# A post-norm decoder on one core: first experts' rows scattered to token order, second context early, another order in self-attention rounds

## The chip, the core and the metric

The kernel runs on one core of a Trainium2 chip. The core has engines with queues of their own: TensorE (PE in the profile, its weight loads PEld) for matmuls and transposes, VectorE (DVE), ScalarE (ACT) and GpSimd (POOL) for elementwise work and reductions, and SyncE (SP), which here only issues DMAs. GpSimd issues the indirect DMAs, which gather or scatter rows by an index. The metric is device time in microseconds (us), as the median of several runs. Next to it stands one profiled execution with a record of each instruction.

## The reference

The input is x of 8 x 256 tokens with 256 features and a context of 8 x 77 tokens with 192. Six sublayers follow one another, and after each comes a layer norm of the sum with its input:

```python
x = _layernorm(x + _L0_attn_ref(x, ...))             # gated linear attention
x = _layernorm(x + _L0_xattn_ref(x, ctx_768, ...))   # 16 heads over the context
x = _layernorm(x + _L0_ffn_ref(x, ...))              # 8 experts, 2 for each token
x = _layernorm(x + _L1_attn_ref(x, ...))             # 16 heads, window of 128 on each side
x = _layernorm(x + _L1_xattn_ref(x, ctx_768, ...))   # logits clipped at 10000
x = _layernorm(x + _L1_ffn_ref(x, ...))              # 8 experts with limited room
```

In the first experts each token has two experts with softmax weights, and each computes `(silu(x W1) * (x W2)) W3`. The second experts use `silu(x w1 + b1) w2 + b2`.

## The kernel before

All of x stays on chip as 16 chunks of 128 tokens, two for each batch, with a transposed copy xT. All is fp32 but for masks, one-hots and softmax shifts in bf16.

**Order of work.** An attention stage is a list of (function, ahead, arguments); `round_of(steps, b)` calls each for batch b + ahead, so that one round works on several batches at once. The text sets the order in which instructions are given. The framework then fixes the order in each engine's queue: nearly always that of the text, but an instruction may pass one whose inputs are expected later. Each queue runs in that order, so an instruction that waits holds up all behind it. PSUM has eight buffers, shared by all stages (`ps`).

**First experts, `ffn0`.** Routing sorts the 2 x 2048 choices by expert into 39 blocks of 128 rows (NB0). For block i, `fetch` gathers its rows from DRAM on GpSimd four blocks ahead, `turn_rows` transposes them (pt_g), `hidden` makes p_u and p_v (L1013), `turn_hidden` transposes their product (pt_h), and `output` makes p_y (L1035) one block later. VectorE copies it to yo (L1040, three buffers), and SyncE stores it to the DRAM tensor ys at the block's place (L1041).

**Back to tokens, `combine`.** For a batch, four gathers on GpSimd (L896) fetch from ys the rows of two chunks and two choices; VectorE multiplies each by its weight and adds (yc, L909). `norm` takes statistics on VectorE, adds and raises to the power -0.5 on GpSimd (L112, L113), and scales on VectorE (x, L115). `combine` is a step of the self-attention's rounds, three batches ahead; `turn_batch` (pt_x, L129) makes xT of the batch two ahead.

**Self-attention rounds.** A batch's exponentials need a row maximum first. `maxima` makes scores p_s (L681) on top of a mask (L671) and reduces them on VectorE (m, L687): sixteen reductions for each batch, in four calls. `less_max` splits the negated maxima into bf16 parts, transposes them (p_mx, L459), and `shift` adds them to the transposed scores p_st that `weigh` makes for the exponentials e on ScalarE (L703). `average` multiplies by the values (p_pv), `divide` divides, `turn` and `project` bring back rows, and `norm_batch` adds and norms. `values` makes p_v of the next batch, and VectorE adds the bias into vals (L659). A round below runs from one p_mx to the next.

**Cross-attention, `xattn`.** `context` makes the keys (p_k, four parts; copied by ScalarE at L542 and VectorE at L545) and values (p_v, one part for each batch) of the context, as a step of the rounds two batches ahead. The second one's weights, w_x1, are loaded after the first experts. Its rounds also hold the routing of the next experts: `choose`, `place` and `enter` (p_tok).

**Second experts, `ffn1`.** Here the output already goes by an indirect DMA on GpSimd (L1115) to token order, and plain loads of 512 KB (L1145, SyncE) bring it back once all 20 scatters have landed. Unused places of a block go to rows after the tokens' (`dump`).

## Time and profile before

| what | value |
|---|---|
| median of 3 runs | 1300.39 us (1299.35 to 1302.56) |
| profiled execution, its own time | 1301.57 us |
| its span | 1299.8 us |
| granted TensorE clock, mean | 0.888 of full speed |
| TensorE busy | 1054.2 us, 81% of the span |
| VectorE busy | 655.3 us, 50% |
| ScalarE busy | 448.4 us, 34% |
| GpSimd busy | 339.9 us, 26% |
| last p_y of the first experts starts | 707.10 us |
| first p_mx of the self-attention | 763.38 us |
| first p_mx of the second cross-attention | 1026.86 us |
| first load back in the second experts | 1263.86 us |

The span runs from the first to the last instruction; the execution's own time is a little longer. A row of a timeline gives start, duration, engine, line, operation, what is written and read, and in brackets how long the engine had been idle before it and what ended that. "<-issue" stands for idle time for which the profile shows no wait. An engine's share of the whole span is a mean over stages with different limits, so that a change in one stage is read from that stage.

### The profile page before, as it was taken

The page shows a single profiled execution, that of the slowest core. Times are in us where ns is not written, and L with a number is a line of the kernel's source. Part 1 is how long each engine was busy: PE and PEld are TensorE (multiplying, and loading weights), DVE is VectorE, ACT ScalarE, POOL GpSimd, SP SyncE. Part 2 cuts the span into 40 slices and gives each one's busy share as a digit, 9 for nine tenths or more (in the row PEclk, how much of TensorE's full clock was granted, in tenths as well). Part 3 has the DMA queues.
Part 4 walks back from the last instruction along what each step waited for, and adds up shares of the span by engine and source line. Part 5 has one row for each costly group of instructions (what it writes and reads, how often), then busy time and mean ns, then how long its engine had stood idle before and what let it go on. Part 6 is the DMA issues. An engine that isn't in the chain of part 4 may idle for free.

```text
span 1299.8 us, 25292 instructions
## 1 busy us (share of the span) xinstructions
PE 1054.2 (81%) x10221; PEld 692.1 (53%) x10221; DVE 655.3 (50%) x1833; ACT 448.4 (34%) x874; POOL 339.9 (26%) x454
## 2 busy tenths in 40 slices
PE   6888888888898649999997468888998888873870
PEld 4556665665665426666665235555555555652540
DVE  6667676654555432222222544444444566764325
ACT  3445454424444212212121134333443444330104
POOL 7545555430111021111111730000000110101544
PEclk9789988889999659999999689899999998975895
DMA  7000000003111291111111210000000010105425
GB/s 191 3 2 2 3 3 2 2 3 130 34 33 34 61 303 45 49 41 49 45 45 57 77 49 2 1 1 1 2 1 1 2 33 18 34 24 150 138 82 174
DMA packets 54517, 62.64 MB, mean 48 GB/s; under 512 B 10897, under 2 KB 45858, under 8 KB 54402
## 3 DMA queue, kind: packets, MB, share of 16 engines
q1 hardware_dynamic: 46368, 44.59, 10.6%
q0 software_dynamic: 5616, 15.34, 4.2%
q8 instruction: 82, 1.34, 0.4%
q10 hardware_dynamic: 2418, 1.09, 0.4%
q14 instruction: 33, 0.27, 0.1%
HBM read 42.78 MB, written 18.22 MB: 47 GB/s over the span
## 4 chain that ended last, share of the span: by engine, by line
PE 56%; DVE 24%; ACT 5%; POOL 5%; issue 4%; DMA 4%; SPq 0%; POOLq 0%; ACTq 0%; DVEq 0%
PE p_y L51 6%; PE p_u L1013 5%; PE p_y L1035 5%; PE p_v L1013 5%; PE p_pv L51 4%; DVE m L687 3%; PE p_q L51 3%; PE p_v L51 3%; PE p_s L681 3%; PE p_st L585 2%; PE p_k L51 2%; PE p_st L696 2%; DVE tot L267 2%; DVE al L275 2%; PE p_s L51 2%
## 5 line engine op out<-in xcount | busy, mean ns | idle before, releaser
L687 DVE TENSOR_REDUCE m<-p_s 128x2 f32<-128x512 f32 x128 | 80.1, 683 | 31.8 <-PE p_s L681 31.8
L1019 DVE TENSOR_TENSOR h<-h,p_v 128x512 f32<-128x512 f32 x39 | 26.8, 688 | 121.1 <-PE p_v L1013 121.1
L896 POOL DMA_INDIRECT xg<-rows,tok x39 | 37.0, 949 | 178.3 <-PE pt_g L1002 158.9
L122 DVE TENSOR_TENSOR y<-p_y,xb 128x512 f32<-128x512 f32 x24 | 16.5, 688 | 118.0 <-PE p_y L51 118.0
L1013 PE MATMUL p_u<-fw,xgT 128*128 x156 | 75.3, 606 | 0.6 <-DVE xgT L1004 0.6
L499 POOL TENSOR_TENSOR xb<-x,L_xattnbo 128x512 f32<-128x512 f32 x16 | 20.3, 1271 | 210.6 <-DVE y L122 169.6
L703 ACT ACTIVATE e<-p_st 128x512 f32<-128x512 f32 x128 | 66.9, 643 | 22.6 <-PE p_st L468 20.2
L1035 PE MATMUL p_y<-fw,hT 128*128 x312 | 73.8, 379 | 0.7 <-ACT hT L1028 0.7
L1013 PE MATMUL p_v<-fw,xgT 128*128 x156 | 74.0, 597 | 0.0
L1035 PEld LDWEIGHTS p_y<-fw,hT 128*128 128x128 f32 x312 | 59.2, 190 | 25.2 <-issue 18.2
L592 ACT ACTIVATE e<-p_st 77x512 f32<-77x512 f32 x128 | 65.7, 600 | 17.7 <-PE p_st L468 17.7
L1028 ACT COPY hT<-pt_h 128x512 f32<-128x512 f32 x39 | 22.8, 585 | 128.7 <-PE pt_h L1026 128.7
L477 ACT COPY u<-p_pv 128x512 f32<-128x512 f32 x48 | 28.1, 585 | 110.9 <-PE p_pv L51 109.9
L51 PE MATMUL p_pv<-e,vals 77*32 77x256 f32 (+1 forms) x1024 | 64.8, 394 | 0.0
L130 ACT COPY xT<-pt_x 128x512 f32<-128x512 f32 x40 | 23.4, 585 | 111.1 <-PE pt_x L129 110.5
L499 POOL TENSOR_TENSOR xb<-x,L_attnbo 128x512 f32<-128x512 f32 x8 | 10.1, 1268 | 189.4 <-DVE y L122 189.4
L129 PE MATMUL pt_x<-ident,x 128*128 128x128 f32 x160 | 28.2, 301 | 37.9 <-DVE x L115 37.5
L576 DVE TENSOR_REDUCE m<-p_s 128x4 f32<-128x308 f32 x128 | 53.0, 467 | 6.9 <-PE p_s L51 6.9
L51 PEld LDWEIGHTS p_pv<-e,vals 77*32 77x32 f32 (+1 forms) x1024 | 33.5, 112 | 32.0 <-issue 18.2
L1013 PEld LDWEIGHTS p_v<-fw,xgT 128*128 128x128 f32 x156 | 30.1, 193 | 38.2 <-issue 38.2
L681 PE MATMUL p_s<-kT,qT 32*128 32x512 f32 x256 | 50.0, 696 | 0.0
L260 POOL TENSOR_TENSOR kl<-kT,be 128x256 f32<-128x256 f32 x56 | 48.2, 861 | 4.4
(271 smaller groups left out, 2420.1 us busy)
## 6 DMA issues: line engine op xcount, KB each, us to landing
fw<-in_L_ffn_W SPq DMA_DIRECT2D x24, 512.0 KB
rows<-x SPq DMA_DIRECT2D x32, 256.0 KB
ys<-yo SPq DMA_DIRECT2D x39, 128.0 KB
m<-in_L_ffn_w SPq DMA_DIRECT2D x16, 256.0 KB
z<-ys SPq DMA_DIRECT2D x8, 512.0 KB
x<-in_x SPq DMA_DIRECT2D x8, 256.0 KB
out<-x SPq DMA_DIRECT2D x8, 256.0 KB
b<-in_L_ffn_b ACTq DMA_DIRECT2D x8, 128.0 KB
```

What stands on the lines that cost most here:

```text
L51: nc.tensor.matmul(dst, l, r, start=(i == 0), stop=(i == n - 1))
L129: nc.tensor.transpose(pt[:, dc, c, :], x[:, 2 * b + c, dc * P:(dc + 1) * P], ident)
L260: nc.gpsimd.tensor_tensor(halves(kls[w][b % 2], w)[:, :, 0, :], halves(kT[b], w)[:, :, 0, :], halves(be, w)[:, :, 0, :], ALU.mult,)
L499: nc.gpsimd.tensor_tensor(xb, x[:, 2 * b:2 * b + 2, :], self.bo.unsqueeze(1).broadcast_to([P, 2, D]), ALU.add)
L576: nc.vector.tensor_reduce(st.less(b)[:, c, j, :], p, AX.X, ALU.max, negate=True)
L592: nc.scalar.activation(e[0:KV].rearrange("p i q -> p (i q)"), p[0:KV].rearrange("p i q -> p (i q)"), AF.Exp)
L681: nc.tensor.matmul(tiles[j].rearrange("p a m -> p (a m)"), st.qT[b][r, t, c * P:(c + 1) * P], kTs[b][r, t, :, :].rearrange("p a m -> p (a ...
L687: nc.vector.tensor_reduce(st.less(b)[:, c, j, 2 * t:2 * t + 2], p, AX.X, ALU.max, negate=True)
L703: nc.scalar.activation(e.rearrange("p i q -> p (i q)"), p.rearrange("p i q -> p (i q)"), AF.Exp)
L896: nc.gpsimd.indirect_dma_start(out=out, out_offset=None, in_=table, in_offset=bass.IndirectOffsetOnAxis(ap=index, axis=0),)
L1013: nc.tensor.matmul(p, xg[:, dc, :], w[:, bass.ds(e * (2 * FF) + dc * FF, FF)], start=(dc == 0), stop=(dc == 1),)
L1035: nc.tensor.matmul(y, hT[:, f * P:(f + 1) * P], w3[:, bass.ds(e * (4 * D) + f * D, D)], start=(f == 0), stop=(f == 3),)
```

## The change

**First experts' output.** `output` no longer stores a block at its place, but scatters its rows with GpSimd to token order, as the second experts do. The addresses dst come from tf, the place of each slot in token order, below zero for an unused slot, which goes to a row of `dump`. In `combine` a batch is now one plain load of 512 KB (z, three buffers, five batches ahead), and the four additions follow three batches ahead, as before. Each load waits for all 39 scatters. `scatter`, `load_back` and `returned` are shared with `ffn1`, whose instructions stay the same.

**Second context.** Making keys and values is split from `xattn` as `xcontext`. For the second cross-attention it is called right after the experts, ahead of the self-attention's rounds, and its weights are loaded behind the experts' own; its rounds then have no `context` steps. For the first one the order stays.

**Order of rounds.** In the self-attention the first `maxima` comes before `values`, another before the first `average`, and both calls of `turn_batch` and the last `maxima` before the second `average`. In the second cross-attention `enter` stands before `project` rather than after it.

```diff
--- before.py
+++ after.py
@@ -419,7 +419,7 @@
         r = []
         for i in range(2):
-            m = pool.tile([P, 2, 4, 32], BF16, tag=f"mx{i}", name=f"mx{i}")
+            m = pool.tile([P, 2, 4, 32], BF16, tag=f"mx{i}", name=f"mx{i}", bufs=1)
             nc.gpsimd.memset(m, 0.0)
             r.append(m)
         return r
@@ -520,13 +520,10 @@
             norm_batch(b, py, xb, self.bk)
-    def xattn(w, ctxT, clamp, es):
+    def xcontext(w, ctxT, es):
+
         wkk, bk, wv, bv = w[2:6]
         kvp = es.enter_context(tc.tile_pool(name="x_kv", bufs=1, reuse_waits="tile"))
-        wk = es.enter_context(tc.tile_pool(name="x_wk", bufs=2, reuse_waits="tile"))
-        st = Steps(w, max_buffers(kvp), wk, wk, clamp)
-
-
         keys = kvp.tile([P, 2, B, 2, KV], F32, tag="keys", name="keys")
         vals = kvp.tile([P, B, H, 32], F32, tag="vals", name="vals")
         nc.gpsimd.memset(vals[:, :, :, DH:32], 1.0)
@@ -563,6 +560,14 @@
             elif b in (0, 2):
                 key_part(part, b // 2)
+        return context, keys, vals
+
+    def xattn(w, given, clamp, es):
+
+        context, keys, vals = given
+        wk = es.enter_context(tc.tile_pool(name="x_wk", bufs=2, reuse_waits="tile"))
+        st = Steps(w, max_buffers(wk), wk, wk, clamp)
+
         def maxima(b, c):
             tiles = [ps.tile([P, 4, KV], F32, tag="ps", name="p_s") for _ in range(4)]
             for t in range(2):
@@ -612,11 +617,10 @@
             (st.queries, 1, 1),
             (weigh, 0, 0),
             (st.turn, -1),
-            (context, 2, 0),
-            (context, 2, 1),
+            *([(context, 2, 0), (context, 2, 1)] if context else []),
             (weigh, 0, 1),
             (st.project, -1),
-            (context, 2, 2),
+            *([(context, 2, 2)] if context else []),
             (maxima, 1, 0),
             (average, 0, 0),
             (average, 0, 1),
@@ -726,14 +730,15 @@
             (weigh, 0, 1, 0),
             (st.project, -1),
             (weigh, 0, 1, 1),
+            (maxima, 1, 0, 0),
             (values, 1),
-            (maxima, 1, 0, 0),
+            (maxima, 1, 1, 0),
             (average, 0, 0),
             (maxima, 1, 0, 1),
+            (turn_batch, -1),
+            (turn_batch, 2),
+            (maxima, 1, 1, 1),
             (average, 0, 1),
-            (maxima, 1, 1, 0),
-            (turn_batch, -1),
-            (maxima, 1, 1, 1),
             (st.divide, 0),
             (st.queries, 2, 0),
         ]
@@ -898,20 +903,52 @@
             in_offset=bass.IndirectOffsetOnAxis(ap=index, axis=0),
         )
-    def combine(b, ys, idx, wgt, wk):
-
-        y = wk.tile([P, 2, D], F32, tag="yc", name="yc")
-        for c in range(2):
-            n = 2 * b + c
-            for k in range(2):
-                yg = wk.tile([P, D], F32, tag=f"yg{k}", name=f"yg{k}")
-                gather(yg, ys, idx[:, k, n:n + 1])
-                nc.vector.scalar_tensor_tensor(
-                    y[:, c, :], yg, wgt[:, k, n:n + 1], y[:, c, :] if k else x[:, n, :], ALU.mult, ALU.add
-                )
-        norm(b, y)
-
-    def ffn0(r, w1, w2, w3, ys, meanwhile):
+    def scatter(table, index, rows, sent):
+        s = nc.gpsimd.indirect_dma_start(
+            out=table, out_offset=bass.IndirectOffsetOnAxis(ap=index, axis=0), in_=rows, in_offset=None,
+        )
+        for other in sent:
+            tc.declare_no_dep(s.ins, other.ins, reason="no two slots go to one place")
+        sent.append(s)
+
+    def load_back(z, rows, sent):
+        s = nc.sync.dma_start(out=z, in_=rows)
+        for other in sent:
+            tc.add_manual_dep(
+                s.ins, other.ins.name,
+                mybir.DependencyInfo(mybir.DependencyClass.Sync, mybir.DependencyReason.DATA),
+                reason="any block may have written these rows",
+            )
+
+    def returned(ys, n):
+
+        return ys[0:2 * NT, :].rearrange("(b c k p) d -> b p (c k) d", c=n, k=2, p=P)
+
+    def combine(ys, sent, wgt, wk):
+
+        zs = {}
+
+        def bring(b):
+            zs[b] = wk.tile([P, 4, D], F32, tag="z", name="z", bufs=3)
+            load_back(zs[b], returned(ys, 2)[b], sent)
+
+        def add(b):
+            z = zs.pop(b)
+            y = wk.tile([P, 2, D], F32, tag="yc", name="yc")
+            for c in range(2):
+                n = 2 * b + c
+                for k in range(2):
+                    nc.vector.scalar_tensor_tensor(
+                        y[:, c, :], z[:, 2 * c + k, :], wgt[:, k, n:n + 1], y[:, c, :] if k else x[:, n, :],
+                        ALU.mult, ALU.add,
+                    )
+            norm(b, y)
+
+        return bring, add
+
+    def ffn0(r, w1, w2, w3, ys, dump, meanwhile):
+
+
         rows = r.rows.rearrange("c k p d -> (c k p) d")
         with ExitStack() as es:
             gp = es.enter_context(tc.tile_pool(name="f_g", bufs=1, reuse_waits="tile"))
...
@@ -958,6 +995,8 @@
                     )
             tf = gp.tile([P, NB0], F32, tag="tf", name="tf")
             tok = gp.tile([P, NB0], I32, tag="tok", name="tok")
+            dst = gp.tile([P, NB0], I32, tag="dst", name="dst")
+            none = gp.tile([P, NB0], F32, tag="none", name="none")
             nc.vector.tensor_scalar(tf, pt[:, NB0:2 * NB0], float(P), -float(P), ALU.mult, ALU.add)
             nc.vector.tensor_tensor(tf, tf, pt[:, 0:NB0], ALU.add)
             nc.vector.tensor_scalar(tok, tf, 0.0, None, ALU.max)
@@ -974,11 +1013,11 @@
             nc.vector.tensor_scalar(bi, be, float(NE - 1), None, ALU.min)
-            idx = r.kept([2, NC], "idx", I32)
             wgt = r.kept([2, NC], "wgt")
             def returns():
-                nc.vector.scalar_tensor_tensor(idx, r.blk, float(P), r.row, ALU.mult, ALU.add)
+                nc.vector.scalar_tensor_tensor(none, tf, 0.0, dump, ALU.is_lt, ALU.mult)
+                nc.vector.tensor_tensor(dst, tf, none, ALU.add)
                 d = gp.tile([P, NC, NE], F32, tag="d", name="d")
                 nc.vector.tensor_tensor(d, r.m[:, 0], r.m[:, 1], ALU.subtract)
                 nc.vector.tensor_tensor(d, d, r.lg, ALU.mult)
...
@@ -1038,18 +1077,17 @@
                     )
                 yo = wk.tile([P, D], F32, tag="yo", name="yo")
                 nc.vector.tensor_copy(yo, y)
-                nc.sync.dma_start(out=ys[i * P:(i + 1) * P, :], in_=yo)
+                scatter(ys, dst[:, i:i + 1], yo, sent)
             for i in range(-4, NB0 + 1):
-                if i == 4:
+                if i == 0:
                     returns()
                 for f, n in ((fetch, i + 4), (hidden, i), (output, i - 1), (turn_hidden, i), (turn_rows, i + 2)):
                     if 0 <= n < NB0:
                         f(n)
-            return idx, wgt
+            return wgt, sent
     def ffn1(r, b1, b2, w1, w2, ys, dump):
-
         rows = r.rows.rearrange("c k p d -> (c k p) d")
         with ExitStack() as es:
...
@@ -1218,7 +1243,7 @@
             )
-    ys = dram.tile([2 * NT + NE * CAP, D], F32, tag="ys", name="ys")
+    ys = dram.tile([2 * NT + P * NB0, D], F32, tag="ys", name="ys")
     right, early = ExitStack(), ExitStack()
     with tc.tile_pool(name="x0_w", bufs=1) as xw:
         lent = {}
@@ -1230,7 +1255,7 @@
             lent["wg0"] = load_k(aw, "wg0", a["L0_ffn_Wg"], NE)
             lent["wg1"] = load_k(aw, "wg1", a["L1_ffn_gate_w"], NE)
             lent["b1"] = load(aw, "b1", a["L1_ffn_b1"], [P, NE, 2], "e (f p) -> p e f", p=P)
-            for n, shape in (("upper", [P, P]), ("iota", [P, P]), ("tid", [P, NC]), ("dump", [P, NB1]),
+            for n, shape in (("upper", [P, P]), ("iota", [P, P]), ("tid", [P, NC]), ("dump", [P, NB0]),
                              ("half", [P, 2]), ("chosen", [P, 4])):
                 lent[n] = load(aw, n, a["c_" + n], shape)
             lent["caps"] = load(aw, "caps", a["c_caps"], [P, 2, 2 * NE], "p (k e) -> p k e", k=2)
...
@@ -1274,37 +1299,41 @@
         load_experts(fw2, FF, "L0_ffn_W2", 2)
         load_experts(fw3, D, "L0_ffn_W3", 4)
         w_s1 = attn_weights(late, "L1_attn", False)
+        w_x1 = attn_weights(late, "L1_xattn", True)
         far = load(late, "far", a["c_far"], [P, 2, P], "p (k s) -> p k s", k=2)
         masks = late.tile([P, 2, P], BF16, tag="masks", name="masks")
         def meanwhile():
             quarter(w_s1)
+            quarter(w_x1)
             nc.vector.tensor_copy(masks, far)
-        idx, wgt = ffn0(r0, fw1, fw2, fw3, ys, meanwhile)
+        wgt, sent = ffn0(r0, fw1, fw2, fw3, ys, dump, meanwhile)
     early.close()
-    late = ctx.enter_context(tc.tile_pool(name="x1_w", bufs=1, reuse_waits="tile"))
-    w_x1 = attn_weights(late, "L1_xattn", True)
     with ExitStack() as es:
         ck = es.enter_context(tc.tile_pool(name="c_wk", bufs=2, reuse_waits="tile"))
         fs = ExitStack()
         steps = self_attn(w_s1, masks, es, fs)
-        steps.insert(4, (lambda b: combine(b, ys[0:NB0 * P, :], idx, wgt, ck), 3))
-        steps.insert(len(steps) - 1, (turn_batch, 2))
-        for b in range(-3, B):
+        bring, add = combine(ys, sent, wgt, ck)
+        steps.insert(4, (add, 3))
+        steps.insert(0, (bring, 5))
+        xs = ExitStack()
+        context, *given = xcontext(w_x1, ctxT, xs)
+        for part in range(3):
+            for b in range(B):
+                context(b, part)
+        for b in range(-5, B):
             run(round_of(steps, b))
-        quarter(w_x1)
         fs.close()
         right.close()
         rest = round_of(steps, B)
-        xs = ExitStack()
-        steps = xattn(w_x1, ctxT, 10000.0, xs)
+        steps = xattn(w_x1, (None, *given), 10000.0, xs)
         run(alternate(rest, round_of(steps, -2) + round_of(steps, -1)))
         rp = right.enter_context(tc.tile_pool(name="r1", bufs=1, side="right", reuse_waits="tile"))
         rw = right.enter_context(tc.tile_pool(name="r1_wk", bufs=2, side="right", reuse_waits="tile"))
         r1 = Route(1, wg1, rp, rw)
         steps.insert(len(steps) - 2, (r1.choose, -1))
-        steps.insert(8, (r1.enter, -2))
+        steps.insert(5, (r1.enter, -2))
         steps.insert(3, (r1.place, -2))
         for b in range(B + 2):
             run(round_of(steps, b))
...
```

More of the change, by code (lines that the diff above doesn't have):

```diff
@@ L943, in ffn0 @@
             for k in range(2):
-                ob = gp.tile([P, NC, NB0], BF16, tag=f"ob{k}", name="ob")
+                ob = gp.tile([P, NC, NB0], BF16, tag="ob", name="ob")
                 o2 = gp.tile([P, NC, 2, NB0], BF16, tag=f"o2{k}", name="o2")
@@ L988, in returns @@
                 meanwhile()
-            raw, xgs, hs, hTs = {}, {}, {}, {}
+            raw, xgs, hs, hTs, sent = {}, {}, {}, {}, []
             def fetch(i):
@@ L1061, in ffn1 @@
             nc.vector.tensor_scalar(src, r.table, -float(P), 0.0, ALU.add, ALU.max)
-            nc.vector.scalar_tensor_tensor(none, r.table, 0.0, dump, ALU.is_equal, ALU.mult)
+            nc.vector.scalar_tensor_tensor(none, r.table, 0.0, dump[:, 0:NB1], ALU.is_equal, ALU.mult)
             nc.vector.scalar_tensor_tensor(dst, r.table, -float(P), none, ALU.add, ALU.add)
@@ L1114, in output @@
                     at += n
-                s = nc.gpsimd.indirect_dma_start(
-                    out=ys, out_offset=bass.IndirectOffsetOnAxis(ap=dst[:, i:i + 1], axis=0),
-                    in_=yo, in_offset=None,
-                )
-                for other in sent:
-                    tc.declare_no_dep(s.ins, other.ins, reason="no two slots go to one place")
-                sent.append(s)
+                scatter(ys, dst[:, i:i + 1], yo, sent)
             for i in range(10):
@@ L1137, in ffn1 @@
                         output(5 * g - 5 + h)
-            back = ys[0:2 * NT, :].rearrange("(b c k p) d -> b p (c k) d", c=4, k=2, p=P)
             yc, stats = {}, {}
@@ L1144, in fetch_pair @@
                 for h in range(2):
-                    s = nc.sync.dma_start(out=z[:, 4 * h:4 * h + 4, :], in_=back[g][:, 4 * h:4 * h + 4, :])
-                    for other in sent:
-                        tc.add_manual_dep(
-                            s.ins, other.ins.name,
-                            mybir.DependencyInfo(mybir.DependencyClass.Sync, mybir.DependencyReason.DATA),
-                            reason="any block may have written these rows",
-                        )
+                    load_back(z[:, 4 * h:4 * h + 4, :], returned(ys, 4)[g][:, 4 * h:4 * h + 4, :], sent)
                 y = wk.tile([P, 4, D], F32, tag="yc", name="yc")
@@ L1255, in decoder_kernel @@
         with ExitStack() as es:
-            steps = xattn(w_x0, ctxT, None, es)
+            steps = xattn(w_x0, xcontext(w_x0, ctxT, es), None, es)
             run(alternate(rest, round_of(steps, -2) + round_of(steps, -1)))
@@ L1345, in _constants @@
         "c_chosen": np.stack([(u[:, 0] % 32 < 12) & (u[:, 0] % 4 == i) for i in range(4)], 1).astype(np.float32),
-        "c_dump": (2 * NT + P + np.arange(P)[:, None] + P * np.arange(NB1)[None, :]).astype(np.float32),
+        "c_dump": (2 * NT + P + np.arange(P)[:, None] + P * np.arange(NB0)[None, :]).astype(np.float32),
         "c_tri": np.ascontiguousarray(np.broadcast_to(tri.reshape(1, NE * NE), (P, NE * NE))),
```

## The prediction

> **What bounds the kernel now.** First the slices: the engine rows by stage. Columns: stretch, length, then busy us (instructions) of TensorE, its weight loads, VectorE, ScalarE, GpSimd, then granted clock, DMA share, GB/s.
>
> ```profile
> 675.00:700.00 25.00, 25.00 (x97) 15.96 (x96) 6.84 (x13) 4.73 (x8) 0.00 (x0) 1.00 0.07 22
> ...
> 709.10:723.67 14.57, 0.00 (x1) 0.01 (x1) 4.45 (x12) 0.00 (x0) 8.95 (x11) 0.58 0.28 81
> 723.67:763.38 39.71, 21.19 (x85) 11.19 (x85) 28.57 (x68) 4.52 (x9) 26.46 (x30) 0.71 0.22 63
> ...
> 833.10:867.50 34.40, 30.66 (x278) 18.39 (x278) 15.92 (x39) 13.98 (x28) 3.12 (x5) 0.95 0.00 1
> ...
> 932.68:963.42 30.74, 28.96 (x279) 18.13 (x279) 14.55 (x33) 13.98 (x28) 2.16 (x3) 1.00 0.01 1
> ```
>
> In the first experts TensorE is full. From their last matmul (709.10) it waits 14.57 us; until the first shift transpose p_mx of self-attention (763.38) it is half busy at a clock of 0.71, and GpSimd and VectorE carry the stage. Then eight rounds follow, from p_mx to p_mx 32.1, 37.6, 34.4, 34.4, 30.8, 30.7, 30.7 and 32.7 us. A steady round holds 28.96 us of TensorE; 34.4 has 3.7 idle and 1.7 from the lower clock.
>
> The timeline says what the gap waits for:
>
> ```profile
> 709.13 0.42 DVE L1040 COPY yo<-p_y 128x256 f32<-128x256 f32 x1 [2.74 <-PE p_y L1035]
> 712.28 1.01 POOL L896 DMA_INDIRECT yg<-ys,idx  x1 [5.96 <-issue]
> ...
> 715.39 0.48 DVE L909 SCALAR_TENSOR_TENSOR yc<-yg,wgt,x 128x256 f32<-128x256 f32 x1 [5.83 <-DMA yg<-ys,idx]
> ...
> 723.67 1.12 PE L129 MATMUL pt_x<-ident,x 128*128 128x128 f32 x4 [14.57 <-DVE x L115]
> ```
>
> Store, landing, a gather every 1.25 us, four per batch, then the norm. In the rounds the chain meets VectorE:
>
> ```profile
> 814.42 2.08 PE L51 MATMUL p_v<-L_attnwv,xT 128*128 128x256 f32 x4 [3.85 <-DVE vals L659]
> ...
> 956.96 4.88 DVE L687 TENSOR_REDUCE m<-p_s 128x2 f32<-128x512 f32 x8 [1.03 <-PE p_s L681]
> ...
> 963.42 0.28 PE L459 MATMUL p_mx<-identb,mx 128*128 128x128 bf16 x2 [1.10 <-DVE mx L456]
> ```
>
> The second p_v waits until VectorE, behind a combine, has taken the first; the last eight maxima queue for 4.88 us just ahead of p_mx.
>
> **Part 1: experts' end.** 39 stores by SyncE become 39 scatters by GpSimd. Price, by the second experts and by the gathers:
>
> ```profile
> L896 POOL DMA_INDIRECT yg<-ys,idx x32: 942/946/1208, 712.3 to 767.3; - x32
> L1115 POOL DMA_INDIRECT ys<-yo,dst x20: 965/971/1002, 1223.9 to 1261.2; - x20
> ```
>
> A block (5.8 us) then holds 0.95 + 0.97 = 1.92 us of GpSimd: hidden behind TensorE; without that cover 39 x 0.97 = 38 us. A gather queued behind a scatter now waits for p_y and its copy, and pt_g for that gather; but gathers are issued four blocks ahead, and nothing else is on the queue except memsets (3.7 us, near 704). The copy into yo waits for the scatter three blocks back, 17 us, against a landing under 2.7. Two small VectorE operations for the addresses replace one; without cover 0.5 us. SyncE's 0.9 MB of cross-attention weights move behind the experts' weights, where SyncE is idle afterwards (DMA share 0.07): nothing; without cover 3 us, at the 303 GB/s of the page's fullest slice.
>
> [...] The trace has 971 ns beside VectorE's bias additions and at most 1208 ns for gathers beside the combine. Its copies in this stage read PSUM, 424 ns. I take 0.97 and nothing[...].
>
> **Part 2: the gap.** The last scatter can start where the store did, 709.6. In the second experts the loads start 1263.86, 2.65 us after the last scatter (1261.21): so 712.3, the time of the first gather now. One load there took 3.8 us to its consumer (ScalarE at 1267.75), the next 1.4 and 1.9 more: data at 716.1, 717.5, 719.4 for batches 0, 1, 2. Three buffers: the fourth waits until batch 0 is added; behind it on SyncE are only the later loads. In the old kernel batch 0 was complete at 723.9.
>
> VectorE now has the context as well: 4 key copies at 0.60 and 8 value copies at 0.42 (as in the rows of keys and vals later) = 5.8 us, in among the first additions. So batch 0 is complete near 726.1, **2.3 us later**; batches 1 and 2, no longer paced by four gathers of 1.25 each plus the norm's GpSimd steps, near 731 and 735 (before 732.5 and 741.2). VectorE's load from the end of the experts to p_mx is 33.0 (both rows) + 5.8 = 38.8 us, from about 712.5: not before 751.3. Written out operation by operation I get p_mx at 754.8, against 763.38: **-8.6 us**. From below: if VectorE waits as often as it does now, 0; from above -12.1.
>
> TensorE's clock: [...] the context's 14.6 us of matmuls fill the gap, and if they keep the clock up, p_v, p_s and the masks before p_mx (7.1 us cold on the chain of waits) take half. [...] VectorE ends last anyway. I take nothing and keep -3.5 for the range.
>
> **Part 3: context leaves the second cross-attention.** Costs now on the path:
>
> ```profile
> 1011.01 2.83 PE L51 MATMUL p_k<-ctxT,L_xattnwk 128*128 128x308 f32 x8
> ...
> 1029.23 2.93 PE L51 MATMUL p_k<-ctxT,L_xattnwk 128*128 128x308 f32 x8
> ```
>
> In the transition p_k and two p_v (1.2 each) stand ahead of pt_o, 5.2 us; TensorE idles 3.6 there for other reasons, so **-4**. In its first round p_k goes, but the p_mx after it follows from y and the norm: **-2**. In rounds 1 to 5 one p_v (1.2) goes; they idle 1.7 to 2.6 us, and the path is y, GpSimd's addition and power, x, transpose: between 0 and -6, I take **-1**. The tokens' p_tok in four rounds now precedes p_y and waits for VectorE's one-hot; p_y, y and the norm queue behind it, some 0.85 us each at worst (+3.4), mostly behind GpSimd's 1.27 us addition: **+0.8**.
>
> **Part 4: order of the rounds.** Eight reductions take 5.4 us per round half; moving two groups of maxima forward gives VectorE work while TensorE averages, and spares the last queue. Ceiling: idle and clock loss of each round against 28.96: 3.1, 8.7, 5.4, 5.4, 1.8, 1.8, and 3.4 in the seventh; 29.6 in all. The waits that the order touches: the p_v wait (3.85 and twice 2.0) in rounds with a combine, and p_mx's wait with the issue gaps after it. I take -2.8, -4.4, -3, -3, -1.2, -1.2, -2.2 = **-18** (61% of the ceiling), because values now come behind four more reductions of 0.68 and average may wait for them; if all of it is lost, 0.
>
> **Sum.** -8.6 - 18 - 4 - 2 - 1 + 0.8 = -32.8. The profiled execution took 1301.57 (span 1299.8, 1.8 around it): 1268.8. The median of the runs is 1300.39, 1.2 lower: 1267.6, say **1268 us**. A difference under 0.3% (3.9 us) can't be told from none.
>
> **Rivals.**
> A. The barrier takes the place of the gathers: all 39 scatters must land and the context stands on VectorE ahead of the adds, so p_mx stays at 763. For it: batch 0 is later even in my count. Against: 32 gathers of 0.95 us leave the stretch. 1268 + 8.6 = 1277.
> B. The new order only exchanges waits: values late, average waits, p_mx as before. For it: VectorE's total is unchanged, and steady rounds are 94% TensorE already. Then -15: 1286. Halfway, 1277.
> C. More: warm clock -3.5, the orders' whole ceiling -11.6, values in the cross-attention -5: to 1248.
> D. Slower: GpSimd becomes the pace of the first experts[...]. It decides where scatter plus gather exceed 5.8 us plus the 32.8/39 = 0.84 that the rest gains: 3.3 us each. At 3.5 each: 7.0 - 5.8 = 1.2 x 39 = +47: 1314. Against: no row over 1.21 us.
> E. It doesn't do what it says: scatters still hold the loads up because landing, not issue, is slow with scattered 1 KB rows. Second experts: 2.65 us with the same rows. At most some 3 more, 1271.
>
> **How the numbers follow.** Mine 50%, A 13%, B 17%, C 11%, D 6%, E 3%. Low end between C and mine, 1251; the high end is B, 1286; outside are D and the ends of B and C, some 2 in 10. Faster by over 0.3%: mine, A, C, E and nearly all of B, 0.90; same: the rest of B with bad p_tok, 0.03; slower: D and a little of B, 0.07.
>
> **What would show it.** Experts still end near 709 and GpSimd's row there is about 8 of 25 us. z loads issue near 712, TensorE's idle of 14.57 is filled by p_k and p_v, pt_x of batch 0 comes at 726 and not before 724, p_mx near 755. Rounds with a combine fall to 31 to 33, the steady ones to 29.5. No p_k after 725; the second cross-attention's start comes 4 us sooner after the last self-attention p_mx. Wrong: a scatter row above 2 us, pt_x after 730, a vals row that average waits for, or rounds that keep 30.7.

## The result, and the profile after

The changed kernel takes 1279.14 us in the median of four runs (1277.38 to 1280.60), against 1299.89 us for the kernel before on the same chip: a ratio of 0.9835, with an interval of 0.982 to 0.985. That is 20.8 us less. The forecast was 1268 us, with 1251 to 1286 around it: right in sign and inside the range, but a gain of 32 us was worked out and two thirds of it came. The profiled execution took 1277.38 us with a span of 1275.5, which is 24.3 under the span before; it was the fastest of its four.

The stage ahead of the experts ends anywhere from 473.0 to 480.2 us in the profiles of this document, with the same work. Places are therefore taken between instructions of one execution. Each step of the forecast against the two profiles (the last p_y is the start of its eight matmuls):

| stretch | before, us | after, us | difference | forecast |
|---|---|---|---|---|
| start of the span to the experts' first pt_g | 475.36 | 476.55 | +1.2 | 0 |
| first pt_g to the last p_y | 231.74 | 231.16 | -0.6 | 0 |
| last p_y to the self-attention's first p_mx | 56.28 | 47.79 | -8.5 | -8.6 |
| its seven rounds | 230.78 | 220.41 | **-10.4** | **-18** |
| to the second cross-attention's first p_mx | 32.70 | 28.29 | -4.4 | -4 |
| its first round | 14.69 | 13.12 | -1.6 | -2 |
| its next six rounds | 113.86 | 116.03 | **+2.2** | **-0.2** |
| from there to the end | 144.39 | 142.15 | -2.2 | 0 |

A second profile of the changed kernel, `after_again`, has the same gap and steady rounds, but 223.1 us in the seven rounds (-7.7) and 114.5 in the six (+0.6): these two rows are known to some 3 and 2 us only. The last row is a sum of two unlike parts: x of the last batch comes 4.3 us later, and the second experts then take 4.6 us less from their first pt_g to their last matmul, though no edit touches them.

The rows by stage of the changed kernel, with the columns as before (stretch, length, busy us of TensorE, its weight loads, VectorE, ScalarE, GpSimd, granted clock, DMA share, GB/s):

```profile
675.00:700.00 25.00, 25.00 (x96) 15.74 (x95) 6.83 (x13) 4.73 (x8) 3.89 (x4) 1.00 0.06 22
...
709.70:726.98 17.28, 14.88 (x50) 5.50 (x48) 9.39 (x24) 2.44 (x4) 2.44 (x4) 1.00 0.40 130
726.98:755.50 28.52, 19.00 (x84) 10.25 (x85) 26.13 (x68) 4.52 (x9) 7.07 (x10) 0.83 0.24 74
...
784.44:821.73 37.29, 33.64 (x280) 19.50 (x279) 18.19 (x48) 13.77 (x28) 3.12 (x5) 0.86 0.01 2
821.73:854.88 33.15, 30.53 (x280) 18.83 (x278) 16.17 (x41) 13.77 (x28) 3.12 (x5) 0.95 0.00 1
...
917.47:946.93 29.46, 28.74 (x279) 18.12 (x278) 14.70 (x35) 13.77 (x28) 2.16 (x3) 1.00 0.00 1
```

The experts are still full on TensorE, with the scatters in GpSimd's column. The gap behind them is filled by the context, and from 727 on VectorE is busy for 26.13 of 28.52 us. The steady rounds fell from 30.74 to 29.46. The second round, the longest, is as long as it was (37.6 and 37.3).

The timeline of the gap (start, duration, engine, line, operation, and in brackets the idle time before it and what ended it):

```profile
709.54 5.68 PE L51 MATMUL p_k<-ctxT,L_xattnwk 128*128 128x308 f32 x16
...
710.44 0.98 POOL L907 DMA_INDIRECT ys<-yo,dst  x1 [0.36 <-DVE yo L1079]
...
715.15 9.43 PE L51 MATMUL p_v<-L_xattnwv,ctxT 128*77 128x256 f32 x32
...
719.11 0.47 DVE L941 SCALAR_TENSOR_TENSOR yc<-z,wgt,x 128x256 f32<-128x256 f32 x1
...
726.98 0.67 PE L129 MATMUL pt_x<-ident,x 128*128 128x128 f32 x4 [2.40 <-DVE x L115]
...
755.50 0.37 PE L459 MATMUL p_mx<-identb,mx 128*128 128x128 bf16 x2 [6.05 <-DVE mx L456]
```

This is what was forecast: batch 0 at 726 to 727, later than before, and p_mx near 755. The loads were issued at 713.27. The price of a scatter was right as well; here are all 59 of both expert layers:

```profile
L907 POOL DMA_INDIRECT ys<-yo,dst x59: 965/987/1002, 492.3 to 1237.7; - x59
```

Now the second round, where the forecast had -4.4:

```profile
798.39 0.74 DVE L115 TENSOR_SCALAR x<-y,mv,rs 128x256 f32<-128x256 f32 x2 [0.82 <-POOL rs L113]
...
800.42 0.73 DVE L115 TENSOR_SCALAR x<-yc,mv,rs 128x256 f32<-128x256 f32 x2 [1.13 <-POOL rs L113]
801.19 0.88 DVE L941 SCALAR_TENSOR_TENSOR yc<-z,wgt,x 128x256 f32<-128x256 f32 x2
801.99 0.87 DVE L941 SCALAR_TENSOR_TENSOR yc<-z,wgt,yc 128x256 f32<-128x256 f32 x2
...
802.92 0.67 DVE L691 TENSOR_REDUCE m<-p_s 128x2 f32<-128x512 f32 x1
...
803.64 0.37 PE L675 MATMUL p_s<-masks,identb 128*128 128x256 bf16 x1 [3.64 <-DVE m L691]
...
805.94 2.08 PE L51 MATMUL p_v<-L_attnwv,xT 128*128 128x256 f32 x4
...
809.96 3.66 PE L51 MATMUL p_pv<-e,vals 128*32 128x256 f32 x32
```

The combine (x of one batch, the additions of another) still stands ahead of everything that TensorE needs from VectorE. Before, p_v waited 3.85 us for vals; now the mask of the second `maxima` waits 3.64 us for the first reduction. Then TensorE runs slowly, at a granted clock of 0.50 for ten us (803.64 to 813.70): a p_v takes 2.08 us here, 1.13 ahead of the wait at a clock of 1.00, and p_pv 3.66 against 1.97 behind it.

### The profile page after: what moved, and what is told of

The parts are those of the page before. It is cut to its first block, busy times and chain, and to the rows that moved or that the text cites. A ratio compares the mean times of both kernels' runs of the same rounds, so it can differ in the third digit from the quotient of the medians.

```text
span 1275.5 us, 25238 instructions
## 1 busy us (share of the span) xinstructions
PE 1057.5 (83%) x10221; PEld 690.5 (54%) x10221; DVE 655.6 (51%) x1834; ACT 447.6 (35%) x874; POOL 348.5 (27%) x461
## 4 chain that ended last, share of the span: by engine, by line
PE 57%; DVE 21%; POOL 6%; issue 6%; ACT 5%; DMA 3%; SPq 1%; POOLq 0%; ACTq 0%; DVEq 0%
PE p_u L1052 5%; PE p_y L1074 5%; PE p_v L1052 5%; PE p_y L51 5%; PE p_q L51 4%; PE p_pv L51 3%; PE p_v L51 3%; PE p_st L590 2%; DVE m L691 2%; PE p_k L51 2%; PE p_st L700 2%; PE p_s L685 2%; PE pt_x L129 2%; DVE tot L267 2%; DVE al L275 2%
## 5 line engine op out<-in xcount | busy, mean ns | idle before, releaser
L907 POOL DMA_INDIRECT ys<-yo,dst x59 | 57.9, 981 | 158.1 <-DVE yo L1079 142.1
L499 POOL TENSOR_TENSOR xb<-x,L_attnbo 128x512 f32<-128x512 f32 x8 | 10.4, 1300 | 191.3 <-DVE y L122 189.5
L112 POOL TENSOR_SCALAR rs<-mv 128x2 f32<-128x2 f32 x40 | 9.6, 239 | 155.5 <-DVE mv L111 155.1
L129 PE MATMUL pt_x<-ident,x 128*128 128x128 f32 x160 | 28.0, 304 | 28.9 <-DVE x L115 28.5
L1052 PEld LDWEIGHTS p_v<-fw,xgT 128*128 128x128 f32 x156 | 29.9, 192 | 37.9 <-issue 37.9
```

Source lines behind the costliest of these rows:

```text
L129: nc.tensor.transpose(pt[:, dc, c, :], x[:, 2 * b + c, dc * P:(dc + 1) * P], ident)
L499: nc.gpsimd.tensor_tensor(xb, x[:, 2 * b:2 * b + 2, :], self.bo.unsqueeze(1).broadcast_to([P, 2, D]), ALU.add)
L907: s = nc.gpsimd.indirect_dma_start(out=table, out_offset=bass.IndirectOffsetOnAxis(ap=index, axis=0), in_=rows, in_offset=None,)
L1052: nc.tensor.matmul(p, xg[:, dc, :], w[:, bass.ds(e * (2 * FF) + dc * FF, FF)], start=(dc == 0), stop=(dc == 1),)
```

## The experiments

The medians, each with its ratio to the kernel before on the same chip; differences of kernels of different chips are read from the ratios (0.001 is 1.3 us).

| run | median, us | ratio | interval |
|---|---|---|---|
| old_rounds | 1289.25 | 0.9927 | 0.9900 to 0.9954 |
| rounds_alone | 1290.40 | 0.9929 | 0.9902 to 0.9957 |
| ctx_back | 1284.38 | 0.9891 | 0.9866 to 0.9919 |
| enter6 | 1276.84 | 0.9824 | 0.9790 to 0.9858 |
| add_late | 1256.95 | 0.9677 | 0.9654 to 0.9700 |
| scatter_alone | 1282.37 | 0.9877 | 0.9855 to 0.9900 |
| sbuf_copies | 1278.57 | 0.9839 | 0.9818 to 0.9861 |
| ctx_back_e8 | 1280.38 | 0.9846 | 0.9828 to 0.9863 |
| after_again | 1278.80 | 0.9836 | 0.9818 to 0.9853 |
| add_late_enter6 | 1253.36 | 0.9631 | 0.9610 to 0.9653 |
| add_late_ctx_back | 1250.38 | 0.9620 | 0.9601 to 0.9639 |
| filler | 1259.45 | 0.9660 | 0.9637 to 0.9684 |

### What is the new order worth?

`old_rounds` is the changed kernel with the list of rounds as it was; `rounds_alone` is the kernel before with the new list.

```diff
--- after.py
+++ old_rounds.py
-            (maxima, 1, 0, 0),
             (values, 1),
-            (maxima, 1, 1, 0),
+            (maxima, 1, 0, 0),
             (average, 0, 0),
             (maxima, 1, 0, 1),
+            (average, 0, 1),
+            (maxima, 1, 1, 0),
             (turn_batch, -1),
-            (turn_batch, 2),
             (maxima, 1, 1, 1),
-            (average, 0, 1),
             (st.divide, 0),
+            (turn_batch, 2),
```

> The changed kernel with the self-attention rounds in their old order; the scatter, the loads back and the early context stay. Theory 1 (the order gives some 1.3 us in every round and nothing more in the rounds with a combine, because VectorE's combine then holds up the masks instead of p_v): rounds go back to about 32, 37.6, 34.4, 34.4, 30.7, 30.7, 30.7 from the first p_mx, the first p_mx moves by at most 3 us, and the time is 9 to 12 us above the changed kernel, near 1289. Rival (the order is worth its 18 us, but scatter and loads took some of it back by pushing the combine into the rounds): 15 to 20 us above, near 1296, with the second round near 41.

> The kernel before with the new order of self-attention rounds alone. Theory 1: 9 to 12 us under the kernel before, near 1290, the second to fourth round gaining no more than 2 us each. Rival (the order's full worth shows only where gathers, not loads, feed the combine): 15 to 18 us under, near 1283. Third possibility (the order needs the loads: four gathers on GpSimd delay the combine, which now stands ahead of the maxima): under 5 us.

Without the order the time is 10 to 12 us higher (by medians and by ratios), and the order alone is worth about 9: theory 1 both times, not the 18 us of the forecast. The rounds of `old_rounds` were 31.3, 37.9, 36.0, 34.4, 30.8, 30.7, 30.8; those of `rounds_alone` 29.5, 35.9, 34.1, 34.1, 29.5, 29.5, 29.0. So the order gives 1.3 us in a steady round, and 0.3 to 2.9 in the second to fourth, which hold a combine, whether gathers or loads feed it. What TensorE waited for in the second round, first in `old_rounds`, then in the changed kernel (wait, us in total, times, longest):

```profile
PE p_v L51 <- DVE vals L663: 3.8, 1, 3.8
```

```profile
PE p_s L675 <- DVE m L691: 3.6, 1, 3.6
```

One wait took the other's place.

### Is it the combine?

If so, the same combine at another place must free those rounds. Between a round's division and its y, VectorE was idle for 10 us. `add_late` puts the additions of batches 3 to 7 there, by an order among VectorE's own instructions.

```diff
--- after.py
+++ add_late.py
+    last = {}
...
-                nc.vector.tensor_tensor(
+                last[0] = nc.vector.tensor_tensor(
                     o[:, c], pt[:, :, 0:DH], rc.unsqueeze(2).broadcast_to([P, H, DH]), ALU.mult
                 )
...
-                    nc.vector.scalar_tensor_tensor(
+                    s = nc.vector.scalar_tensor_tensor(
...
+                    if b > 2:
+                        tc.add_manual_dep(
+                            s.ins, last[0].ins.name,
+                            mybir.DependencyInfo(mybir.DependencyClass.NoSync, mybir.DependencyReason.DATA),
+                            reason="behind the division",
+                        )
...
-        steps.insert(4, (add, 3))
+        steps.append((add, 3))
```

> The changed kernel with the combine of batches 3 to 7 (additions and norm) placed on VectorE behind the division of the round, where VectorE is idle for 10 us ahead of y, instead of behind y and ahead of the maxima. Theory 1 (in the second to fourth round the combine ahead of the maxima is what holds TensorE at the masks and then halves its clock): the second round falls from 37.3 to 30 to 31 us, the third and fourth from 33.1 to about 30, and the first p_mx comes 4 to 7 us sooner since only three batches are combined ahead of it: 14 to 20 us under the changed kernel, near 1262. Rival (those rounds are long for TensorE's clock and work, and the wait only goes to the next reduction or to y): under 5 us.

It took 1256.95 us, some 21 us under the changed kernel (0.9677 against 0.9835), a little more than expected. Its stretches from p_mx to p_mx, and the start of the second round on VectorE:

```profile
748.58:777.32 28.74, 28.40 (x262) 16.80 (x263) 11.39 (x23) 13.75 (x26) 0.00 (x0) 0.94 0.00 1
777.32:806.80 29.48, 28.76 (x279) 18.15 (x279) 18.07 (x46) 13.78 (x28) 3.09 (x5) 1.00 0.06 20
806.80:836.26 29.46, 28.75 (x279) 18.12 (x278) 17.88 (x45) 13.78 (x28) 3.09 (x5) 1.00 0.06 19
```

```profile
777.47 0.75 DVE L497 TENSOR_TENSOR o<-pt_u,rc 128x256 f32<-128x256 f32 x2
...
778.14 0.87 DVE L943 SCALAR_TENSOR_TENSOR yc<-z,wgt,x 128x256 f32<-128x256 f32 x2
778.93 0.87 DVE L943 SCALAR_TENSOR_TENSOR yc<-z,wgt,yc 128x256 f32<-128x256 f32 x2
...
781.81 0.73 DVE L115 TENSOR_SCALAR x<-yc,mv,rs 128x256 f32<-128x256 f32 x2 [1.13 <-POOL rs L113]
```

VectorE does as much in the second round as before (18.07 us, 18.19 in the changed kernel), and the round falls from 37.3 to 29.5. TensorE's busy time falls with it, from 33.64 to 28.76: of the 7.8 us, 4.9 were matmuls at the lowered clock (0.50) behind the wait, 2.9 idle time. All seven rounds fall to 205.0 from 220.4, and the first p_mx comes 41.2 us after the last p_y instead of 47.8, since only three batches are combined ahead of it. In those rounds the place of the combine is thus the cause, not its amount.

### The scatter and the early context

`ctx_back` makes keys and values in the cross-attention again, as the kernel before did. `scatter_alone` has the old rounds as well, with p_tok where the kernel before had it.

```diff
--- after.py
+++ ctx_back.py
-        for part in range(3):
-            for b in range(B):
-                context(b, part)
...
-        steps = xattn(w_x1, (None, *given), 10000.0, xs)
+        steps = xattn(w_x1, (context, *given), 10000.0, xs)
...
-        steps.insert(5, (r1.enter, -2))
+        steps.insert(7, (r1.enter, -2))
```

> The changed kernel with keys and values of the second context made in the cross-attention again, as in the kernel before; their weights stay loaded behind the experts. Theory 2 (in the gap the context's VectorE copies stand among the first additions and delay batch 0): without them x of batch 0 is ready near 722 instead of 726.4, the first p_mx comes 3 to 5 us sooner, TensorE is cold again there (clock near 0.7 from 709 to 755), and the transition and first round of the cross-attention get their 6 us back: 1 to 4 us above the changed kernel. Rival (the context in the gap is free and keeps TensorE's clock up, so that p_mx comes no sooner without it): 6 to 10 us above the changed kernel.

> The scatter and the plain loads back alone: the changed kernel with the old order of rounds and with the second context in the cross-attention (its weights stay loaded behind the experts). If the three parts add up, 20.8 less 10.1 less 5.2: some 5 to 6 us under the kernel before, near 1294, with x of batch 0 as early as 721.5 after the experts' end at 709.5 but the first p_mx no sooner than 46 us after the last p_y. Rival (parts overlap in the gap: without the context the loads alone are worth the whole 10 us there): near 1289.

`ctx_back` is 5.2 us above the changed kernel by the medians, between its two expectations, and 7.3 by the ratios, within the rival's. Its gap:

```profile
721.54 1.12 PE L129 MATMUL pt_x<-ident,x 128*128 128x128 f32 x4 [12.04 <-DVE x L115]
...
753.77 0.37 PE L459 MATMUL p_mx<-identb,mx 128*128 128x128 bf16 x2 [5.63 <-DVE mx L456]
```

Counted from the last p_y, x of batch 0 was turned 5.2 us sooner than with the early context (14.0 against 19.3), but p_mx only 1.5 us sooner (46.3 against 47.8). Between the two the clock was 0.71, against 0.83 with the early context, and VectorE was still waited for at the end. The transition and first round cost 31.9 and 16.4 us, against 28.3 and 13.1: 6.9 us, as the forecast had it (6).

`scatter_alone` was a surprise: 16.5 us under the kernel before, where 5 to 6 were expected if parts add up, and below the rival's 1289 too. In its profile the gap gave 11.0 us (45.3 against 56.3), and the stretch behind the last p_mx 6.1, of which 4.4 lie in the second experts, which no edit touches. The three parts do not add up, and the early context beside old rounds seemed to cost 6 us. One more edit stood between these runs, though: p_tok.

### Where p_tok stands, and the context once more

`enter6` puts p_tok behind p_y; `ctx_back_e8` is `ctx_back` with p_tok behind p_y; `add_late_enter6` and `add_late_ctx_back` are the late combine with p_tok behind p_y, with and without the early context.

```diff
--- after.py
+++ enter6.py
-        steps.insert(5, (r1.enter, -2))
+        steps.insert(6, (r1.enter, -2))
```

> The changed kernel with the tokens' matmuls p_tok of the second routing behind p_y, where they were, instead of ahead of it. Theory 3 (p_tok ahead of p_y waits for VectorE's one-hots and delays y in four rounds): 2 to 5 us under the changed kernel, the rounds of 19.9 and 21.2 us falling to about 18.5. Rival (GpSimd's addition hides it): within 1 us.

> Scatter, loads back and the new order of rounds, with the second context in the cross-attention and p_tok behind p_y, both where they were in the kernel before: the one part missing against the kernel with p_tok behind p_y is the early context. If the early context is worth its 4 to 6 us (3.6 in the transition, 3.2 in the first round, less 1.5 in the gap): 1281 to 1283, above the kernel with p_tok behind p_y at 1277. If it costs as it seemed to with the old rounds (1282 without against 1289 with it): near 1272. If the earlier difference lay in p_tok standing ahead of p_y while the context is in those rounds: about 5 us under the 1284 of the run with the context back, and the cross-attention's seven rounds at 128 us instead of 133.

> The changed kernel once more, on the chip of the other three: 1276 to 1281, as the yardstick for their differences.

> The late combine with p_tok behind p_y. If p_tok's place costs nothing, as the run with that edit alone showed (2 us, inside its spread): 1255 to 1259, as the late combine alone at 1257. If it costs 2 to 5 us once the other waits are gone: 1252 to 1255.

> The late combine with the second context in the cross-attention and p_tok behind p_y. If the early context is worth 4 to 6 us: 1261 to 1263. With VectorE relieved in the gap, the context's copies there cost less, so that its worth could rise to the whole 6.8 us of transition and first round: 1264. If the early context costs 2 to 6 us in truth: 1251 to 1255.

With p_tok behind p_y the ratio falls from 0.9891 to 0.9846 without the early context, and from 0.9677 to 0.9631 with the late combine; in both pairs the intervals just fail to meet, the kernels ran on different chips, and the difference is about 6 us by the ratios and 4 by the medians. In the changed kernel itself (0.9835 to 0.9824) nothing can be told: the runs of `enter6` spread over 11 us. So p_tok ahead of p_y costs time in two of three surroundings. In the seven rounds the profiles show it in one pair only (`ctx_back_e8` 130.5 us, not the 128 expected, against 133.0; with the late combine 132.6 and 132.5). Behind the last p_mx they all show it: from there to the last pt_x it is 29.9 to 30.1 us in the eight profiles with p_tok behind p_y, the kernel before among them, and 32.4 to 34.4 in the six with p_tok ahead. The last round of `add_late`, then of `add_late_enter6`:

```profile
1138.56 0.21 PE L51 MATMUL p_tok<-o,oh 128*128 128x40 bf16 x1 [1.79 <-DVE o L871]
1138.60 1.20 PE L51 MATMUL p_y<-L_xattnwo,oT 128*128 128x256 f32 x2
```

```profile
1139.43 3.78 PE L51 MATMUL p_y<-L_xattnwo,oT 128*128 128x256 f32 x8 [0.67 <-ACT oT L514]
```

Ahead of p_y, p_tok waits for VectorE's one-hots, and p_y behind it; behind p_y it leaves p_y to start as soon as ScalarE has copied oT. That is theory 3, where no other work covers the wait.

With p_tok behind p_y and the context in the cross-attention, the new order on top of the scatter also shows alone: 0.9877 to 0.9846, about 4 us, with intervals that overlap, although the seven self-attention rounds fall by 9.5 us in the profiles (231.4 to 221.9). Why the rest doesn't come through stays open.

The early context is worth nothing that can be measured: with p_tok at one place, 0.9824 with it and 0.9846 without, intervals overlapping, and with the late combine 0.9631 with it and 0.9620 without, on the same chip. The two profiles of the late combine show what it gives and takes (the one with the early context is the slowest of its five runs). With the early context: -4.0 in the transition and -2.1 in the first round of the cross-attention, but +4.5 in the gap, +1.6 in the first self-attention round, and +6.0 in the last six rounds of the cross-attention (119.9 against 113.9), which have *less* to do. In the pair with the early combine these six grow too, from 114.2 (`ctx_back_e8`) to 117.4 (`enter6`, whose profile is slower than its median too). Rounds two, three and six of the cross-attention, `add_late_enter6` and then `add_late_ctx_back`:

```profile
997.33:1014.35 17.02, 13.82 (x147) 9.82 (x147) 10.56 (x32) 7.55 (x15) 2.21 (x3) 0.90 0.10 33
1014.35:1035.75 21.40, 18.39 (x163) 13.91 (x163) 12.47 (x42) 7.78 (x16) 2.21 (x3) 0.76 0.08 25
...
1075.43:1095.99 20.56, 17.34 (x157) 11.59 (x158) 14.46 (x62) 7.56 (x15) 2.16 (x3) 0.80 0.09 28
```

```profile
998.38:1014.64 16.26, 13.69 (x150) 9.34 (x150) 10.97 (x33) 7.54 (x15) 2.20 (x3) 1.00 0.11 34
1014.64:1033.33 18.69, 16.48 (x167) 11.68 (x167) 12.77 (x43) 7.77 (x16) 2.20 (x3) 0.91 0.09 29
...
1072.62:1090.78 18.16, 15.55 (x162) 10.22 (x162) 14.80 (x63) 7.54 (x15) 2.18 (x3) 1.00 0.10 31
```

With four matmuls less in a round, TensorE is busy longer, at a clock of 0.75 to 0.90 where it was 0.91 to 1.00. The third round shows how, again without and then with p_v in it:

```profile
1025.35 1.01 PE L131 MATMUL pt_x<-ident,x 128*128 128x128 f32 x4 [1.37 <-DVE x L115]
...
1027.64 3.58 PE L51 MATMUL p_l<-wg,xT 128*128 128x8 f32 x16
```

```profile
1021.52 1.18 PE L51 MATMUL p_v<-L_xattnwv,ctxT 128*77 128x256 f32 x4
...
1025.72 0.67 PE L131 MATMUL pt_x<-ident,x 128*128 128x128 f32 x4 [0.43 <-DVE x L115]
...
1027.44 1.95 PE L51 MATMUL p_l<-wg,xT 128*128 128x8 f32 x16
```

The next x comes 6.0 us behind the start of p_y in both, so that p_v had filled a wait. Without it the wait is 1.37 us instead of 0.43, and p_l behind it takes 3.58 us; with p_v p_l takes 1.95. The mean clock of the round is 0.76 and 0.91.

### Is it the clock?

`filler` gives TensorE those matmuls back and nothing to the other engines.

```diff
--- add_late_enter6.py
+++ filler.py
+        def filler(b):
+            p = ps.tile([P, D], F32, tag="ps", name="p_f")
+            s = slice(b * KV, (b + 1) * KV)
+            mm(p[0:KV, :], [(ctxT[:, 0, s], w[4][:, 0, :]), (ctxT[0:64, 1, s], w[4][0:64, 1, :])])
...
-            *([(context, 2, 2)] if context else []),
+            (context, 2, 2) if context else (filler, 2),
```

> The late combine with the early context and p_tok behind p_y, and in the second cross-attention's rounds one added pair of matmuls for each batch where the context's p_v stood, of the same shape and inputs, whose result nobody reads: TensorE has more to do and no other engine has. Theory 4 (taking p_v out of these rounds lets TensorE idle long enough that its clock is lowered, and that costs more than the 1.2 us of each p_v): the granted clock there rises from 0.75 to 0.90 towards 0.91 to 1.00, the seven rounds fall from 132.6 to 129 to 130.5 us (the first round still has no p_k), and the time is 2 to 4 us under the 1253.4 of the same kernel without the added matmuls. Rival (the clock has nothing to do with it, the rounds are long for other reasons): the rounds grow by up to 7 us and the time is 1254 to 1261.

```profile
997.95:1014.44 16.49, 14.08 (x150) 9.63 (x151) 10.66 (x32) 7.55 (x15) 2.17 (x3) 1.00 0.10 33
1014.44:1034.63 20.19, 18.28 (x166) 13.39 (x166) 12.55 (x42) 7.78 (x16) 2.17 (x3) 0.85 0.08 27
...
1074.39:1092.55 18.16, 15.55 (x162) 10.23 (x162) 14.49 (x62) 7.55 (x15) 2.18 (x3) 1.00 0.09 31
```

The clock rose (0.90, 0.76, 0.80 to 1.00, 0.85, 1.00), and the last six rounds fell from 119.9 to 116.0 with more work in them. That part of theory 4 is shown, in one profile each; `add_late`, whose profile is the median of its runs, has 119.8 in the six. But the matmuls that also went into the transition (+2.1) and the first round (+1.7, where the clock fell from 1.00 to 0.86) took the gain back, and the time was not lower: a ratio of 0.9660 against 0.9631, intervals overlapping. As a way to a faster kernel the filler failed.

### Copies beside the scatters

The forecast took 0.97 us for a scatter and nothing more. `sbuf_copies` asks whether that holds beside more work on VectorE: it puts eight copies from one on-chip buffer to another behind each block's copy into yo.

```diff
--- after.py
+++ sbuf_copies.py
                 nc.vector.tensor_copy(yo, y)
+                idle = wk.tile([P, P], F32, tag="idle", name="idle", bufs=1)
+                for _ in range(8):
+                    nc.vector.tensor_copy(idle, yo[:, 0:P])
                 scatter(ys, dst[:, i:i + 1], yo, sent)
```

> The changed kernel with eight added VectorE copies of 128 x 128 fp32 from one on-chip buffer to another behind each block's copy into yo, so that they run beside GpSimd's scatter and the next gather; their result isn't used. [...] By the trace so far no scatter is longer than 1.0 us. Either way the time stays within 2 us of the changed kernel; if GpSimd becomes the pace of the experts, it is over 10 us more.

```profile
L907 POOL DMA_INDIRECT ys<-yo,dst x59: 965/987/1002, 493.7 to 1241.7; - x59
...
L1082 DVE COPY idle<-yo x312: 215/227/2586, 493.5 to 716.0; 128x128 f32<-128x128 f32 x156
...
639.15 0.99 POOL L907 DMA_INDIRECT ys<-yo,dst  x1 [3.55 <-DVE idle L1082]
639.69 2.02 DVE L1082 COPY idle<-yo 128x128 f32<-128x128 f32 x6
640.44 0.97 POOL L901 DMA_INDIRECT xg<-rows,tok  x1 [0.30 <-issue]
```

The scatter and the gather run amid the copies and are no longer for it: scatters take 0.987 us in the median and 1.002 at most, gathers 0.970 and 1.084, against 0.987, 1.002, 0.970 and 1.085 in the changed kernel. The time is that of the changed kernel too (a ratio of 0.9839 against 0.9835). It is a copy that gets longer: in 37 of the 39 scatters, and in all 31 gathers that had copies beside them, the copy that starts 0.54 to 0.56 us into the transfer takes 0.44 to 0.47 us instead of 0.22 to 0.24, and ends within 0.04 us of it. The longest copy, 2.59 us, began during a scatter and went on beside a memset of 1.82 us on GpSimd. So in this run the added time falls on VectorE. Longer copies were not tried.

## Why the prediction was right or wrong

- **Experts' end (part 1): right.** A scatter was forecast at 0.97 us and hidden; it took 0.987, and the stage got 0.6 us shorter. Rival D, the slower side, fell with it.
- **The gap (part 2): right, by its own steps.** Loads at 713.3 after experts that ended 0.6 later (forecast 712.3), pt_x at 726.98, p_mx at 755.5 (754.8). VectorE was the bound from pt_x on (26.1 of 28.5 us), though its work in the gap was 35.5 us and not the 38.8 counted; `add_late`, which takes work from it, got another 6.6 us there. The choice to take nothing for the clock was sound in the sum, but not in its parts: the context delayed batch 0 by 5.2 us and p_mx by 1.5 only, and the clock rose from 0.71 to 0.83 meanwhile.
- **The order of the rounds (part 4): wrong by 7.6 us, or 10 in the second profile.** The failed step is "-4.4, -3, -3" for the rounds with a combine: gains of 0.3, 1.3 and 1.3 came, in `after_again` 0.4 and then none. The forecast named the right wait (p_v behind a combine) and moved p_v behind four reductions, but did not ask what those reductions stand behind. It was the same combine, so that the wait went to the mask (3.64 us where it was 3.85) and slow matmuls followed as before (p_v 2.08 us in both). This is rival B, confined to three rounds. The steady rounds were right (-1.3 each, forecast -1.2).
- **The context out of the cross-attention (part 3): right where it was costed, wrong where it was waved through.** Transition and first round gave 4.4 and 1.6. For the other rounds the sum took -1 for p_v and +0.8 for p_tok: +2.2 came, +0.6 in `after_again`. It named the path of these rounds rightly (y, addition, power, x), but the bounds of 0 and -6 were set as if fewer matmuls could only help; p_v filled a wait on that path, and two pairs of profiles show the six rounds 3 and 6 us longer without it. And p_tok, taken at +0.8 and bounded at +3.4, costs 4 to 6 us in two pairs of runs, 2.3 to 4.3 of it behind the last p_mx.
- **The likeliest case and its range.** The time lies between the forecast and its rival B. In the profiles luck has a part in it: behind the last p_mx, second experts that took 4.6 us less, though no edit touches them, covered what p_tok cost there. The part that was expected to matter most, the order, brought 10.4 of the 24.3 us in the profile; by the runs the scatter alone brings 16.5 us, and the early context none.

The experiments led to a better kernel: scatter and loads back, the new order, a late combine, and context and p_tok as they were before. `add_late_ctx_back` takes 1250.38 us, 0.962 of the kernel before (0.9601 to 0.9639), 28 us under the changed kernel.

## What to carry to other kernels

When a reordering is to remove a wait on an in-order engine, write down what stands ahead of the new head of the queue: if it is the same slow group, the wait only changes its name (here 3.85 us for vals became 3.64 us for a reduction), and it is that group which has to move, into a stretch where its engine is idle. Matmuls that leave a stage in which TensorE already waits need not be a gain by their duration: here 1.2 us of them less in a round went with up to 2.7 us more. See first what they fill, and what the granted clock does after the waits of that stage. And when several edits come together, run each without the others, and some in pairs: here one brought 16 us alone, one 9 alone and about 4 on top of the first, one nothing, and a small one in their shadow cost time.

## What the runs showed of the hardware that was not expected

In the second self-attention round of the changed kernel a wait of 3.64 us on TensorE cost more than itself: for the ten us after it the granted clock was 0.50 (p_v 2.08 us for 1.13, p_pv 3.66 for 1.97), and the round held 4.9 us more of busy time than the same round without the wait (33.64 us, 28.76 in `add_late`). Shorter waits were followed by slow matmuls as well. In the third round of the changed kernel they were 1.81 and 0.81 us, with matmuls between them, and then the clock was 0.54 for 3.75 us (p_v 2.08 again); in the third cross-attention round of `add_late_enter6` it was one of 1.37 us (p_l 3.58 for 1.95). What else these places have in common was not tested, and how long a wait has to be for this was not shown. In rounds two to six of the cross-attention `add_late_enter6` has four matmuls of 1.2 us in all less than `add_late_ctx_back`: there the mean granted clock of a round was 0.75 to 0.90 instead of 0.91 to 1.00, and a round took up to 2.7 us longer.

In `sbuf_copies`, beside GpSimd's indirect DMAs (0.987 us in the median for a scatter, 0.970 for a gather), one VectorE copy for each took some 0.24 us longer in 37 of 39 scatters and 31 gathers, and the DMAs took no longer than in the changed kernel.
